# Cross-attention block on one core: one pair fewer turned on TensorE, later layer norm statistics, earlier fc weights, and weight sums at the head of their pair

## The chip, the core and the metric

The kernel runs on one core of a Trainium2 chip. The metric is the device time of one execution in microseconds (us); the median of several runs counts. The engines are named as in the profile: PE is TensorE, DVE is VectorE, ACT is ScalarE, POOL is GpSimd, SP is the engine that here only issues transfers.

## The reference

All data are float32. B = 4 batches, 512 queries and 512 keys of width D = 512, H = 16 heads of 32, and a hidden layer of 2048.

```
y = layer_norm(x)                     # ln1
q = y @ q_w + q_b;  k = ctx @ k_w + k_b;  v = ctx @ v_w + v_b
attn = softmax(mask(q k^T / sqrt(32)))
h = (attn v) @ cproj_w + cproj_b + x
out = h + gelu(layer_norm(h) @ fc_w + fc_b) @ proj_w + proj_b
```

## The kernel before, in words

**Windows, units and pairs.** The 16 heads of a batch make 4 groups, so there are 16 windows w = 4 * batch + group. A window has four query tiles qt of 128; unit u is 4 * w + qt, 64 in all. Two units make a pair: pair p is window p // 2, half p % 2. In this text "(w,qt)" names a unit and batch numbers count from 0, so "batch two" of the change is batch 1.

**One unit.** `scores` (L227) multiplies one query tile with all keys for four heads into PSUM (tile `sc`, one buffer), DVE adds the mask and takes the minimum (L239, output `s`), and ACT takes the exponential with the row sum (L243). The probabilities must then be transposed for the product with v. `turn` (L247) does this in one of two ways. For most pairs DVE transposes blocks of 32x32 (L271, tile `tb`), and when the pair is full its reciprocal sums are added (L276 to L279) and `copies` (L299) issues 16 transfers on SP (L313) that move the blocks to their places in `pT`. For the pairs listed in `ON_PE`, TensorE transposes instead (L257, tile `tpp`), DVE and ACT copy the result out of PSUM (L260, L262), and `turn_sums` (L326) transposes the sums (tile `tpr`).

**Where a pair is put.** `pT` has one buffer, so `exchange` (L288) lets only one pair at a time hold it (list `held`) and makes the next wait until `attend` (L336) has used it. A pair listed in `IN_G` goes into the buffer `gt` instead, which later holds the hidden layer and, at the end, fc's weights; it doesn't wait for `pT`. `attend` of pair p runs at the start of unit 2p + 4, except for the pairs that `AT` places by hand. Its product is tile `av` (L356).

**The order of the other work.** All engines follow the program's order (the schedule is written by hand). Into the units, each window w spreads the list `first[w]` (from its third unit on also `later[w]`): the projections `prep_k`, `prep_q`, `prep_v` of coming windows, the layer norm of coming batches, the output projection `cproj` and the first two batches' MLP. Each entry has a cost (3.4 for a chain of matmuls, 0.5 for a turn of the layer norm, 0 for the rest), and every unit takes entries twice, before and after its `turn`, while half of the next cost fits into the share due. `inputs(b)` returns four groups for batch b: x1 loads x, x2 is layer norm 1 in three parts (statistics of tiles 0 and 1; statistics of tiles 2 and 3 with the reciprocal root on POOL; the four normalizations L127), x3 is four turns (transposes L136 on PE, eviction with weight and bias on ACT or DVE, L139 and L141), x4 loads the context. `hid_` loads the residual of batch 0 on the current queue and has POOL add a bias to it (L368); `cproj` adds its product to that tile on DVE (L397).

**Queues.** Loads go through `Q[0]`: POOL's queue in windows 0 to 3, SP's from window 4 on. `load_mlp` (L440) loads as many MLP weights as its 8 buffers take, and is called again after each chain.

**The last two batches' MLP.** `last_mlps` (L513) multiplies 2x2 blocks with seven instead of eight products, from sums of blocks. `fc_pair` (L547) does this for two of fc's 16 weight blocks at a time (8 pairs c per batch): seven products of two matmuls each on PE, sums of the products on DVE, gelu on ACT. The products need sums of the weights: `sum_wa` (L509, four DVE instructions, L487 and L490) makes those of pair c + 1 while pair c runs, and `load_wa` (L505) loads those of pair c + 2 when pair c has been issued, into one of two buffers in `gt`.

Of the kernel before, what the change touches and what calls it, by code (L numbers as in the profile page):

```python
# [56 lines left out]
AHEAD = 3  # L57
NORMAL = 2
LAG = 4
IN_G = (2, 5)  # L60
IN_XE = (29, 31)
AT = {7: 1, 9: 2, 13: 4, 15: 5}
ON_PE = (0, 3, 6)
MW = 8
WARM = 14
PW = 2 * NT * HG * HD
# [7 lines left out]
def xattn_block(ctx: ExitStack, tc: tile.TileContext, x, encT, mask, q_w, k_w, v_w, c_w, fc_w, p_w, vecs, rows, out):  # L74
# [32 lines left out]
    def acc_tile(name):  # L107
        return ps_acc.tile([P, D], F32, tag="acc", name=name)
# [71 lines left out]
    def load_w(w, queue=None, names=("wk", "wq", "wv")):  # L180

        if w >= NW:
            return
        g = w % NG
        for n, src in (("wk", k_w), ("wq", q_w), ("wv", v_w)):
            if n in names:
                S[n, w] = (two if n == "wk" else one).tile([P, ND, P], F32, tag=n, name=f"{n}_{w}")
                (queue or Q[0]).dma_start(out=S[n, w], in_=src[:, g, :, :])

    def prep_k(w):  # L190
        b, g = divmod(w, NG)
        kT = kqp.tile([P, L], F32, tag="kT", name=f"kT_{w}")
        acc = acc_tile(f"acck_{w}")
        for d in range(ND):
            nc.tensor.matmul(acc, S["wk", w][:, d, :], eT[:, d, :], start=(d == 0), stop=(d == ND - 1))  # L195
        nc.scalar.activation(kT, acc, AF.Identity, bias=vec[:, KB + g : KB + g + 1], scale=1.0)
        S["kT", w] = kT

    def prep_q(w):
        b, g = divmod(w, NG)  # L200
        qT = kqp.tile([P, L], F32, tag="qT", name=f"qT_{w}")
        acc = acc_tile(f"accq_{w}")
        for d in range(ND):
            nc.tensor.matmul(acc, S["wq", w][:, d, :], xT[:, d, :], start=(d == 0), stop=(d == ND - 1))  # L204
        load_w(w + 1, names=("wq",))

        nc.scalar.activation(qT, acc, AF.Identity, bias=qb[:, g : g + 1], scale=-scale)
        S["qT", w] = qT
# [38 lines left out]
    def turn(w, qt):  # L247

        half, q = divmod(qt, 2)
        if 2 * w + half in ON_PE:  # L250
            if q == 0:
# [36 lines left out]
    def exchange():  # L288

        while waiting:  # L290
            w, half = waiting[0]
            if 2 * w + half not in IN_G + IN_XE:
                if held:
# [5 lines left out]
    def copies(w, half):  # L299
        tb = S["tb", w, half]  # L300

        pair = 2 * w + half
        if pair in IN_G or pair in IN_XE:
            pT = (gt if pair in IN_G else xe).rearrange("p (i n) -> p i n", i=NI)
        else:
# [10 lines left out]
    def over_sums(w, half):  # L316

        if 2 * w + half not in ON_PE:
            return
# [6 lines left out]
    def turn_sums(w, half):  # L326
        if 2 * w + half not in ON_PE:
            return
        tp = acc_tile(f"tpr_{w}_{half}")
        for q in range(2):  # L330
            nc.tensor.transpose(tp[:, ts(q, P)], S["rr", w, half][:, ts(q, P)], ident)
        rb = one.tile([P, 2 * P], F32, tag="rb", name=f"rb_{w}_{half}")
        nc.scalar.copy(rb, tp[:, : 2 * P])
        S["rb", w, half] = rb

    def attend(w, half):  # L336
# [4 lines left out]
        v, pT = S["v", w], S["pT", w, half]  # L341
        on_pe = 2 * w + half in ON_PE
        av = acc_tile(f"av_{w}_{half}")
# [26 lines left out]
    def load_hid(b, ts_):  # L370

        for t in ts_:
            if ("hid", b, t) not in S:
                S["hid", b, t] = hids.tile([P, D], F32, tag="hid", name=f"hid_{b}_{t}")
            Q[0].dma_start(out=S["hid", b, t], in_=S["xa", b][ts(t, P), :] if b else x[b, ts(t, P), :])
        for t in ts_:
            add_row(S["hid", b, t], 1 if b else 0)
# [135 lines left out]
    def last_mlps():  # L513
# [10 lines left out]
        def half_tile(name):  # L524
            return ps_last.tile([P, 2, HL], F32, tag="half", name=name)

        def acc_half(name):
            return acc_tile(name).rearrange("p (i l) -> p i l", i=2)

        def add(engine, o, x0, x1):  # L530
            engine.tensor_tensor(o, x0, x1, ALU.add)

        def y_blocks(b):
            return [S["yT", b][:, 2 * k : 2 * k + 2, j * HL : (j + 1) * HL] for k in range(2) for j in range(2)]

        def p_sums(c):

            c = slice(c, c + 2)
            b11, b12, b21, b22 = (pb[:, c, k, j * HL : (j + 1) * HL] for k in range(2) for j in range(2))
            b_sums(b11, b12, b21, b22, pt[:, 0, c], pt[:, 1, c], b12, pt[:, 2, c])  # L540
# [6 lines left out]
        def fc_pair(b, c, sums):  # L547
            a11, a12, a21, a22 = (wa[c % 2][:, i, 2 * k : 2 * k + 2] for i in range(2) for k in range(2))
            y11, y12, y21, y22 = y_blocks(b)
            s1, s2, s3, s4 = (ws[c % 2][:, i] for i in range(4))  # L550
            t1, t2, t3, t4 = (ys[:, i] for i in range(4))
            q1, q62 = (acc_half(f"{n}_{b}_{c}") for n in ("q1", "q62"))
            q75, q43 = (half_tile(f"{n}_{b}_{c}") for n in ("q75", "q43"))
            p1 = ring.tile([P, HL], F32, tag="p1", name=f"p1_{b}_{c}")
            uc, u34, h = (ring.tile([P, 2, HL], F32, tag=n, name=f"{n}_{b}_{c}") for n in ("uc", "u34", "h"))

            def product(o, a, y):
                for k in range(2):
                    nc.tensor.matmul(o, a[:, k], y[:, k], start=(k == 0), stop=(k == 1))  # L559

            def gelu(i, j, src):
                f = 2 * c + i
                nc.scalar.activation(
                    ga[:, c, i, j * HL : (j + 1) * HL], src, AF.Gelu_apprx_tanh,
                    bias=vec[:, FCB + f : FCB + f + 1], scale=1.0,
                )

            product(q1[:, 0], a11, y11)
            nc.scalar.copy(p1, q1[:, 0])
            product(q62[:, 1], a12, y21)  # L570
            product(q43[:, 1], s4, y22)
            product(q62[:, 0], s2, t2)
            add(nc.vector, uc, q62, p1[:, None, :].broadcast_to([P, 2, HL]))
            gelu(0, 0, uc[:, 1])
            product(q75[:, 0], s3, t3)
            product(q75[:, 1], s1, t1)
            add(nc.vector, u34, q75, uc[:, :1].broadcast_to([P, 2, HL]))
            add(nc.vector, uc[:, 0], q75[:, 1], u34[:, 0])
            gelu(1, 1, uc[:, 0])
            sums()  # L580
            product(q43[:, 0], a22, t4)
            add(nc.vector, h, q43, u34)
            gelu(1, 0, h[:, 0])
            gelu(0, 1, h[:, 1])
# [62 lines left out]
        for b in range(NORMAL, B):  # L647
# [15 lines left out]
            def sums(b=b):  # L663
                if b == NORMAL:
                    for c in range(0, NP, 2):
                        p_sums(c)
                if b + 1 < B:
                    load_hid(b + 1, range(NT))
# [16 lines left out]
    def do(fn):  # L685
        return [(0.0, fn)]

    def A(w):
        if w >= NW:
            return []  # L690
        return do(lambda: load_w(w + 1, names=("wk",))) + [
            (CHAIN, lambda: prep_k(w)),
            (CHAIN, lambda: prep_q(w)),
            (CHAIN, lambda: prep_v(w)),
        ]

    def C(b):
        return [(CHAIN, lambda t=t: cproj(b, t)) for t in range(NT)]
# [4 lines left out]
    def turns2(b):  # L703
        return [(TURN, lambda d=d: ln2_turn(b, d)) for d in range(ND)]
# [7 lines left out]
    def inputs(b):  # L712
        ln = [(0.0, lambda part=part: ln1(b, part)) for part in range(3)]
        return do(lambda: load_x(b)), ln, turns1(b), do(lambda: load_enc(b))
# [38 lines left out]
    first = [[] for _ in range(NW)]  # L753
    later = [[] for _ in range(NW)]
    x1, x2, x3, x4 = inputs(1)
    load2, k2, q2, v2 = A(2)
    load3, k3, q3, v3 = A(3)
    load4, k4, q4, v4 = A(4)
    first[0] = do(lambda: load_w(2, names=("wk",))) + [(CHAIN, lambda: prep_v(1)), (CHAIN, lambda: prep_q(1))] + x1 + [load2, k2, q2]
    first[1] = x2[:1] + [v2] + x2[1:2] + [load3, k3] + x2[2:] + [q3] + x3[:2] + [v3] + x3[2:] + x4  # L760
    first[2] = [load4, q4, k4, v4] + A(5)[:2]
    first[3] = A(5)[2:] + A(6)
    mlp = []
    for p in range(NORMAL):
# [6 lines left out]
    def hid_(b, *ts_):  # L771
        return do(lambda: load_hid(b, ts_))
# [17 lines left out]
    x1, x2, x3, x4 = inputs(2)  # L790
    first[3] += x1
    load, k, q, v = A(7)
    c, t2 = C(0), turns2(0)
    first[4] = do(load_mlp) + [load, k] + x2[:2] + [q] + x2[2:] + [v] + x3[:2] + x4 + hid_(0, 0, 1, 2, 3)
    later[4] = c[:1] + x3[2:] + c[1:] + rs(0)
    load, k, q, v = A(8)
    first[5] = norm(0, 0, 1) + [load, q] + norm(0, 2, 3) + [k] + t2 + [v] + do(lambda: proj_bias(0)) + some(5)
    load, k, q, v = A(9)
    x1, x2, x3, x4 = inputs(3)
    first[6] = [load, k, q] + some(5) + [v] + x1  # L800
    load, k, q, v = A(10)
    first[7] = [load, k, q] + some(5) + [v]

    load, k, q, v = A(11)
    first[8] = ct(1) + [load, k] + x2[:1] + [q] + x2[1:2] + some(1) + x2[2:] + [v] + x3[:2] + x4
    c = C(1)
    later[8] = c[:1] + x3[2:] + c[1:]
    load, k, q, v = A(12)
    first[9] = [load, q] + some(2) + [k] + some(3) + [v]
    load, k, q, v = A(13)  # L810
    first[10] = [load, k, q] + some(5) + [v] + yn(1)
    load, k, q, v = A(14)
# [4 lines left out]
    load, k, q, v = A(15)  # L817
    c = C(2)
# [98 lines left out]
```

## Time and profile before

| | |
|---|---|
| median of 3 runs | 842.71 us (839.12 to 842.92) |
| profiled execution: its time, its span | 844.56 us, 842.7 us |
| mean granted TensorE clock | 0.994 |
| PE busy | 818.0 us (97%) |
| DVE busy | 551.0 us (65%) |
| ACT busy | 345.0 us (41%) |
| POOL busy | 104.8 us (12%) |
| transposes of pairs on TensorE (L257) | 96 records, 282 ns each |
| block transposes on DVE (L271) | 232, 684 ns each |
| transfers of pairs on SP (L313, to pT) | 400 of 136 KB, 2.4 us to landing |

The span runs from the first to the last instruction of the profiled execution. A busy time is the time in which the engine had an instruction under way; those of PE overlap, so the starts of two instructions tell more than the length of one. The number in brackets at the end of a line of the timeline is the idle time before that work and what ended it.

### The profile page before, as it was taken

What the parts mean: (1) busy time and instruction counts of PE and PEld (TensorE: products, weight loads), DVE (VectorE), ACT (ScalarE), POOL (GpSimd) and SP (SyncE); (2) the same over time, 40 slices, a digit from 0 to 9 for tenths busy, and PEclk for the clock granted to TensorE, in tenths of its full rate; (3) what the DMA queues carried; (4) which work ended last, traced back from release to release, by engine and by line L of the source; (5) the groups of instructions that cost most, each with busy time, mean ns of one, the idle gap of its engine ahead of it and who ended that gap; (6) DMA issues with size and microseconds to landing.
All of it is one profiled execution on the core that took longest, in us unless ns stands there. A gap on an engine that the chain in (4) does not pass through costs nothing.

```text
span 842.7 us, 12030 instructions
## 1 busy us (share of the span) xinstructions
PE 818.0 (97%) x4098; PEld 476.6 (57%) x4098; DVE 551.0 (65%) x1254; ACT 345.0 (41%) x745; POOL 104.8 (12%) x124
## 2 busy tenths in 40 slices
PE   9988999989999999999999999999998999999998
PEld 7545555535444554354454444444446788887887
DVE  3595959596766686766886576777136886358511
ACT  2655555336663663456334285556002321023200
POOL 2311212222000021000100310000203012100011
PEclk9998999999999999999999999999999999999999
DMA  5455574957767686886769697857726450022001
GB/s 204 164 146 133 148 203 113 330 136 185 185 168 231 177 250 166 196 211 172 223 174 257 166 238 173 238 138 185 215 88 208 153 163 14 26 75 81 8 14 38
DMA packets 58909, 134.66 MB, mean 160 GB/s; under 512 B 11888, under 2 KB 14064, under 8 KB 58720
## 3 DMA queue, kind: packets, MB, share of 16 engines
q1 hardware_dynamic: 55440, 122.86, 53.6%
q0 software_dynamic: 2880, 9.90, 3.7%
q10 hardware_dynamic: 528, 1.14, 0.6%
q8 instruction: 33, 0.54, 0.3%
q14 instruction: 28, 0.23, 0.1%
HBM read 61.89 MB, written 7.34 MB: 82 GB/s over the span
## 4 chain that ended last, share of the span: by engine, by line
PE 83%; DVE 9%; DMA 4%; SPq 2%; issue 1%; ACT 1%; POOL 0%; DVEq 0%; ACTq 0%; POOLq 0%
PE accp L465 13%; PE accf L455 12%; PE av L356 7%; PE sc L234 7%; PE q L559 6%; PE accv L216 6%; PE acck L195 5%; PE accq L204 5%; PE accc L396 5%; SPq L313 2%; DVE gt L487 2%; PE q4p L595 2%; PE q3p L595 2%; PE q6p L595 2%; PE q1p L595 2%; PE q5p L595 2%
## 5 line engine op out<-in xcount | busy, mean ns | idle before, releaser
L243 ACT ACTIVATE s<-s,mn 128x512 f32<-128x512 f32 x256 | 181.7, 711 | 173.2 <-DVE mn L239 173.0
L239 DVE CUSTOM_DVE_ANT_0 s<-sc,mb 128x512 f32<-128x512 f32 x256 | 161.3, 686 | 49.9 <-PE sc L234 49.8
L271 DVE STREAM_TRANSPOSE tb<-s 128x512 f32<-128x512 f32 x232 | 147.7, 684 | 5.0 <-ACT s L243 5.0
L455 PE MATMUL accf<-yT,fcw 128*128 128x512 f32 x256 | 114.9, 599 | 0.0
L465 PE MATMUL accp<-pw,gt 128*128 128x512 f32 x256 | 114.3, 598 | 0.0
L455 PEld LDWEIGHTS accf<-yT,fcw 128*128 128x128 f32 x256 | 47.1, 190 | 65.0 <-issue 60.8
L465 PEld LDWEIGHTS accp<-pw,gt 128*128 128x128 f32 x256 | 47.4, 190 | 63.2 <-issue 60.7
L234 PE MATMUL sc<-kT,qT 32*128 32x512 f32 x512 | 73.2, 641 | 3.0 <-DVE mn L239 2.2
L356 PE MATMUL av<-pT,v 128*32 128x256 f32 x896 | 57.2, 398 | 7.4 <-DMA pT<-tb 4.9
L216 PEld LDWEIGHTS accv<-wv,xe 128*128 128x128 f32 x512 | 58.9, 192 | 8.9 <-issue 6.7
L216 PE MATMUL accv<-wv,xe 128*128 128x128 f32 x512 | 60.6, 277 | 0.0
L195 PE MATMUL acck<-xe,wk 128*128 128x512 f32 x128 | 58.7, 601 | 0.0
L559 PE MATMUL q<-ys,gt 128*128 128x256 f32 x256 | 57.9, 379 | 0.7 <-issue 0.7
L204 PE MATMUL accq<-xe,wq 128*128 128x512 f32 x128 | 58.5, 599 | 0.0
L396 PE MATMUL accc<-wc,oT 128*128 128x512 f32 x128 | 57.0, 597 | 0.0
L559 PE MATMUL q<-yT,gt 128*128 128x256 f32 x192 | 47.4, 385 | 5.6 <-DVE gt L487 5.5
L559 PEld LDWEIGHTS q<-ys,gt 128*128 128x128 f32 x256 | 48.6, 190 | 7.6 <-issue 1.0
L356 PEld LDWEIGHTS av<-pT,v 128*32 128x32 f32 x896 | 28.0, 113 | 37.4 <-issue 22.3
L243 ACT ACTIVATION_READ_ACCUMULATOR s<-s,mn 128x1 f32 x256 | 47.9, 187 | 0.0
L469 DVE TENSOR_TENSOR hid<-accp,hid 128x512 f32<-128x512 f32 x32 | 21.9, 685 | 39.7 <-PE accp L465 39.7
L223 POOL TENSOR_TENSOR v<-v,row 128x512 f32<-128x512 f32 x16 | 20.5, 1279 | 205.2 <-ACT v L221 205.0
L559 PEld LDWEIGHTS q<-yT,gt 128*128 128x128 f32 x192 | 35.3, 190 | 15.6 <-PE q L559 7.0
(121 smaller groups left out, 865.7 us busy)
## 6 DMA issues: line engine op xcount, KB each, us to landing
pT<-tb SPq DMA_DIRECT2D x400, 136.0 KB, 2.4
fcw<-fc_w_dram SPq DMA_DIRECT2D x32, 256.0 KB, 3.2
pw<-p_w_dram SPq DMA_DIRECT2D x32, 256.0 KB, 3.5
gt<-fc_w_dram SPq DMA_DIRECT2D x32, 256.0 KB, 2.8
gt<-tb SPq DMA_DIRECT2D x32, 136.0 KB, 3.4
pb<-p_w_dram SPq DMA_DIRECT2D x16, 256.0 KB, 3.8
xe<-tb SPq DMA_DIRECT2D x24, 136.0 KB, 2.4
xe<-encT_dram SPq DMA_DIRECT2D x12, 256.0 KB, 5.9
```

Of the source, the lines that this page charges most:

```text
L195: nc.tensor.matmul(acc, S["wk", w][:, d, :], eT[:, d, :], start=(d == 0), stop=(d == ND - 1))
L204: nc.tensor.matmul(acc, S["wq", w][:, d, :], xT[:, d, :], start=(d == 0), stop=(d == ND - 1))
L216: nc.tensor.matmul(acc[:, ts(t, P)], eT[:, d, ts(t, P)], S["wv", w][:, d, :], start=(d == 0), stop=(d == ND - 1),)
L234: nc.tensor.matmul(sc[:, h, :], qT[r, ts(qt, P)], kT[r, :], start=True, stop=True)
L239: nc.vector.tensor_tensor_reduce(out=s, in0=sc[:, h, :], in1=S["mb", w // NG], scale=1.0, scalar=FMAX, op0=ALU.add, op1=ALU.min, accum_out=mn,
L243: nc.scalar.activation(s, s, AF.Exp, bias=mn, scale=-1.0, accum_out=sums[:, qt, h : h + 1])
L271: nc.vector.transpose(tv[:, q, h], S["ps", w, qt][h])
L356: nc.tensor.matmul(av[ts(h, HD), : 2 * P].rearrange(shape, **kw), v[:, t, ts(h, HD)], p[t][h], start=(t == 0), stop=(t == NT - 1),)
L396: nc.tensor.matmul(acc, S["oT", b][:, g, ts(t, P)], wc[:, g, :], start=(g == 0), stop=(g == NG - 1))
L455: nc.tensor.matmul(acc, S["fcw", b, f][:, d, :], S["yT", b][:, d, :], start=(d == 0), stop=(d == ND - 1))
L465: nc.tensor.matmul(acc, gT[q % 2][:, k, ts(t, P)], S["pw", b, q * FQ + k], start=(k == 0), stop=(k == FQ - 1))
L559: nc.tensor.matmul(o, a[:, k], y[:, k], start=(k == 0), stop=(k == 1))
```

## The change

It makes five edits. The pair 6 (window 3, first half) leaves `ON_PE`, so it is transposed by DVE and moved by SP into `pT`. The pair 7 is put into `gt`. In window 1, the parts of layer norm 1 of batch 1 move behind other entries of the list, all four turns come after `prep_v(3)`, and the context's load stands ahead of them. The first eight MLP weights are loaded at the start of window 2 instead of window 4, which also puts them on POOL's queue instead of SP's. In `fc_pair` the sums of the next pair's weights stand first, and the product with s4 moves from the third to the sixth place in every pair but the first of a batch.

```
-IN_G = (2, 5)
+IN_G = (2, 5, 7)
...
-ON_PE = (0, 3, 6)
+ON_PE = (0, 3)
...
+            sums()
             product(q1[:, 0], a11, y11)
             nc.scalar.copy(p1, q1[:, 0])
             product(q62[:, 1], a12, y21)
-            product(q43[:, 1], s4, y22)
+
+            if c == 0:
+                product(q43[:, 1], s4, y22)
             product(q62[:, 0], s2, t2)
...
             gelu(1, 1, uc[:, 0])
-            sums()
+            if c:
+                product(q43[:, 1], s4, y22)
             product(q43[:, 0], a22, t4)
...
-    first[1] = x2[:1] + [v2] + x2[1:2] + [load3, k3] + x2[2:] + [q3] + x3[:2] + [v3] + x3[2:] + x4
-    first[2] = [load4, q4, k4, v4] + A(5)[:2]
+    first[1] = x2[:1] + [v2, load3, k3] + x2[1:2] + [q3] + x2[2:] + [v3] + x4 + x3
+    first[2] = do(load_mlp) + [load4, q4, k4, v4] + A(5)[:2]
...
-    first[4] = do(load_mlp) + [load, k] + x2[:2] + [q] + x2[2:] + [v] + x3[:2] + x4 + hid_(0, 0, 1, 2, 3)
+    first[4] = [load, k] + x2[:2] + [q] + x2[2:] + [v] + x3[:2] + x4 + hid_(0, 0, 1, 2, 3)
```

## The prediction

> **What bounds the kernel now.** I read the busy times first, then the waits of each engine, then the timelines of PE, DVE and SP around the edits.
>
> ```profile
> PE 818.0 (97%) x4098; PEld 476.6 (57%) x4098; DVE 551.0 (65%) x1254; ACT 345.0 (41%) x745; POOL 104.8 (12%) x124
> ```
>
> PE bounds the whole, so an edit gains what it takes off PE, or a hole that it closes in PE's row. The holes lie in three places. In window 1 and at pair 6 (PE, starts and lengths in us):
>
> ```profile
> 60.38 1.14 PE L234 MATMUL sc<-kT,qT 32*128 32x512 f32 x8 [2.18 <-DVE mn L239]
> ...
> 66.98 2.07 PE L257 MATMUL tpp<-ident,s 128*128 128x128 f32 x12 [1.83 <-ACT s L243]
> ...
> 112.84 0.66 PE L257 MATMUL tpp<-ident,s 128*128 128x128 f32 x4 [0.50 <-ACT qT L207]
> ...
> 120.04 1.91 PE L257 MATMUL tpp<-ident,s 128*128 128x128 f32 x16
> ```
>
> In window 4 PE waits twice for a pair's transfers:
>
> ```profile
> 155.05 1.93 PE L356 MATMUL av<-pT,v 128*32 128x256 f32 x32 [1.72 <-DMA fcw<-fc_w_dram]
> ...
> 177.85 3.39 PE L356 MATMUL av<-pT,v 128*32 128x256 f32 x32 [3.72 <-DMA pT<-tb]
> ```
>
> SP's own timeline tells why the second is late, and DVE's what else depends on SP there:
>
> ```profile
> 151.41 3.92 SPq L447 DMA_DIRECT2D fcw<-fc_w_dram  x8
> ...
> 157.42 3.09 SPq L149 DMA_DIRECT2D xe<-encT_dram  x4
> 161.35 2.20 SPq L375 DMA_DIRECT2D hid<-x_dram  x4
> ```
> ```profile
> 167.97 0.69 DVE L397 TENSOR_TENSOR hid<-accc,hid 128x512 f32<-128x512 f32 x1 [7.32 <-POOL hid L368]
> ```
>
> Pair 8's transfers follow only at 163.96, behind these loads and after pair 7 has given `pT` back. And DVE stands 7.32 us before batch 0's residual is loaded and biased; everything behind L397 on DVE stands too. At the end, PE waits in each pair of fc's weights for their sums:
>
> ```profile
> 644.42 1.13 PE L559 MATMUL q<-yT,gt 128*128 128x256 f32 x4 [1.80 <-DVE gt L487]
> ...
> 650.93 1.10 PE L559 MATMUL q<-yT,gt 128*128 128x256 f32 x4 [0.21 <-DVE gt L487]
> ```
>
> [...] it grants 0.50 from 68.95 to 75.75 us and from 178.2 to 181.5 us, after the holes above. [...] the blocks of (4,2) could be transposed at 162, and start at 170.22 behind L397. [...] 3.92 us of SP for eight loads; on POOL one issue takes 0.55 us.
>
> **Part by part.**
>
> *Layer norm in window 1.* The statistics of tiles 2 and 3 (2 x (0.66 + 0.18), 1.6 us start to start) leave the place ahead of L239 of (1,1), which starts at 56.2 instead of 57.8; PE's scores of (1,2) come at 58.8. They return ahead of L239 of (1,2), but the normalizations (1.8) leave there: it starts at 63.6 instead of 65.3, and tpp at 65.25 instead of 66.98: −1.7. From tpp to the scores of (2,0) PE took 83.37 − 66.98 = 16.4 us, 6.8 of them at half clock. With smaller holes I take full clock: −3.0 more (half of 6.8 is 3.4; waits give some back). The normalizations now stand ahead of L239 of (1,3), under PE's product for pair 1 and v: they end about when its scores do. Turns and context load only change places; the same counts, and POOL has nothing between: 0. If that cover went, the 1.8 us would be PE's. Sum −4.7, from −1.7 (clock falls anyway) to −4.7.
>
> *Weights earlier.* 8 x 0.55 = 4.4 us of POOL in window 2. Behind them in POOL's queue stand wk of window 5, wq, wv and v's bias (1.28 us each), none needed for 10 us; 2 MB beside a DMA share of 0.54 to 0.61. 0, at worst +1. On SP, eight issues go: priced below.
>
> *Pair 6.* PE loses two tpp groups of 1.75 us start to start, the 0.50 wait and the sums' 0.3: −4.3. DVE loses 4 copies of 0.69 and gains 8 transposes, 2.4 us per four, and 0.4 for sums: +2.4, beside at least 8 us of DVE idle time between 111 and 134; free. If DVE were full it would cost 2.4. SP gets 16 issues, 10.6 us. On the new clock pair 5's issues run 103.9 to 114.5, pair 6's blocks and sums are done at 115.1, issues end at 125.8, and the row of before gives 2.3 to 3.9 us to landing: 128.1 to 129.6. PE wants them at 136.94 − 4.7 − 4.3 − 0.3 = 127.6. A new wait of 0.5 to 2; I take 1.2. So the product for pair 6 starts at 128.8 instead of 136.94: −8.1.
>
> *Window 4: pair 8 passes the residual's load.* This is where I expect most of that to be lost. Pair 7 sits in `gt`, so `pT` is free when pair 8 is full, and `turn` of (4,1) issues its 16 transfers at once. The context's and the residual's loads are taken after that `turn`: on SP they move from ahead of pair 8 to behind it. Pair 8's sums ended at 155.7; DVE runs from scores (3,3) to there without a hole, so now at 147.4. Add 10.6 for pair 8, 3.1 for the context and 0.9 between: the residual's issue comes at 162, against 161.35 before, although all else is 8 us sooner. Landing took 5.3 with eleven weight loads ahead; with a lighter queue I take 3.5, then POOL's 1.27: L397 at **167.0**, against 167.97 (bounds 165.5 to 170).
>
> What waits: PE runs on through the output projection's tile 2, but tile 3 needs L397's PSUM buffer, so PE stands from about 161, and its clock falls. That is hidden: DVE needs 22.3 us from L397 to L239 of (5,1) (190.3 − 167.97), PE only some 21 even with the clock at half first. Before, PE came 0.8 later than DVE there because of the 3.72 wait and the half clock; both are gone. From L397 to the product for pair 9 it was 199.45 − 167.97 = 31.5 and is now 30.1: −1.4. With −1.0 for L397 itself: **−2.4 in all up to here**, not −8.1 and the waits too.
>
> *fc's pairs.* Seven products take 28 records of 0.216 us, 6.05 us; pairs take 6.4 to 8.1. Batch 2: 688.85 − 633.77 − 48.4 = 6.7 lost; batch 3: 790.72 − 739.16 − 48.4 = 3.2. The sums (1.5 us) were made from 5 to 7 us after a pair's start and wanted at 6.05 + 1.73 = 7.8. Now they wait only for the next weights: the last block is issued when the pair before ends, 3.0 us to landing, sums done at 4.6; after the sums of gelu's blocks (even pairs, 2.7) and a normalization, at 5.7. Both before 7.8. DVE's sum uc then waits behind them, from 2.6 to 4.6 or 6.4; who waits for it is ACT's gelu, wanted later, and PSUM, two pairs deep: 0. The first pair of batch 2 keeps some 0.9 for the sums of y. Gain 9.9 − 0.9 − 0.4 for what I can't see = **−8.6**; bounds 0 and −9.9. PE runs to the end of the chain, so all of it counts.
>
> Sum: 842.7 − 2.4 − 8.6 = 831.7. The profiled execution's own time (844.56) lies 1.9 above its span, and the median (842.71) on the span by chance; I give 831.7 for the median.
>
> **Rivals.**
>
> *No gate.* The residual lands in time, or DVE recovers. Then the −8.1 stays and the waits 1.72 and 3.72 and 1.7 of half clock go too: −15.2 − 8.6 gives 819. For it: the loads are free to start early. Against: SP's row, in order.
>
> *The end gives nothing.* The wait for sums turns into one for weights, as DVE stands for the load at the head of the pair: 842.7 − 2.4 = 840.3. It would take a landing of over 6 us (7.8 − 1.5 after the issue); 5.2 is the longest in batch 2, 3.0 the median. If only window 1's clock still falls, 834.7.
>
> *Slower, by the gate.* Each us that L397 comes after 169.4 is lost one for one. At the gain of 8.6 it decides from 178.0 on. If each of pair 8's 16 issues took as long as the longest L313 of before (2007 ns), they took 32 us and L397 came 21.5 later, at 188.5: 842.7 + 19.1 − 8.6 = 853. Against: the median issue is 0.59.
>
> **How the numbers follow.** Forecast 0.57, with its own range 828 to 836. No gate 0.17. The end gives nothing, or only the clock falls, 0.15. The slower gate 0.06. The last 0.05 is for what I don't see, on either side. The range 821 to 838 takes the forecast, the way to "no gate" but for its last 2 us, and the half-clock case. About 0.5% (4.2 us) is what a measurement can tell from no change: faster is the forecast, no gate and half of the third, 0.83; same 0.09; slower 0.08.
>
> **What would show it.** The rows L257, L260 and L262 at 64, 8 and 8; PE without 50% clock near 70; a wait of PE for pT near 128; on SP, pair 8's L313 ahead of L149 and L375; a wait of DVE for POOL at L397 of about 15 us and a hole in PE of 5 us or more near 161 to 167; in the pairs of fc no wait of PE for gt L487, and one of DVE for the transfers into gt of 1 to 3 us. I am wrong if L397 comes before 163 or after 170, or if pairs of fc still take over 6.2 us.

## The result and the profile after

| | before | after |
|---|---|---|
| median, us | 842.26 (839.12 to 845.02, 6 runs) | 836.84 (835.47 to 838.42, 6 runs) |
| profiled execution: time, span | 844.56, 842.7 | 838.42, 836.6 |

The ratio of after to before is 0.994, interval 0.9914 to 0.9966. The change makes the kernel faster by 5.4 us (0.6%); 11 were forecast. The direction held, and the median lies within the forecast's range (821 to 838). The size did not hold.

PE was busy for 5.3 us less than the 818.0 of before. The span became 6.1 us shorter:

```profile
PE 812.7 (97%) x4064; PEld 472.9 (57%) x4064; DVE 557.9 (67%) x1259; ACT 342.3 (41%) x740; POOL 109.5 (13%) x132
```

The timeline of PE after the change, at the places that were shown of before (start, length in us; in brackets the idle time before and what ended it):

```profile
59.35 1.14 PE L234 MATMUL sc<-kT,qT 32*128 32x512 f32 x8 [0.61 <-DVE mn L239]
65.72 2.16 PE L257 MATMUL tpp<-ident,s 128*128 128x128 f32 x12 [1.60 <-ACT s L243]
...
110.83 1.93 PE L356 MATMUL av<-pT,v 128*32 128x256 f32 x32 [1.15 <-DMA gt<-tb]
...
133.95 1.93 PE L356 MATMUL av<-pT,v 128*32 128x256 f32 x32 [1.51 <-DMA pT<-tb]
...
172.88 5.63 PE L396 MATMUL accc<-wc,oT 128*128 128x512 f32 x8 [6.70 <-DVE hid L397]
...
201.90 1.93 PE L356 MATMUL av<-pT,v 128*32 128x256 f32 x32
```

The last line is the product for pair 9, which started at 199.45 before the change.

The hole ahead of the scores at 59 us has shrunk from 2.18 to 0.61. Two waits are new, at the products for pair 4 (110.83) and pair 6 (133.95), for their transfers. The two waits in window 4 (1.72 and 3.72) are gone, and one of 6.70 stands in their place. What ends it is L397 on DVE. DVE's timeline, and POOL's for what DVE waits for:

```profile
172.14 0.69 DVE L397 TENSOR_TENSOR hid<-accc,hid 128x512 f32<-128x512 f32 x1 [15.82 <-POOL hid L368]
```
```profile
170.84 4.93 POOL L368 TENSOR_TENSOR hid<-hid,row 128x512 f32<-128x512 f32 x4 [19.96 <-DMA hid<-x_dram]
```

DVE stands for 15.8 us because POOL stands for 20, and POOL waits for the residual's load. SP's timeline says where that load was:

```profile
120.44 10.56 SPq L313 DMA_DIRECT2D pT<-tb  x16
135.29 13.09 SPq L313 DMA_DIRECT2D gt<-tb  x16
...
152.88 11.36 SPq L313 DMA_DIRECT2D pT<-tb  x16
164.29 2.02 SPq L149 DMA_DIRECT2D xe<-encT_dram  x4
166.36 1.85 SPq L375 DMA_DIRECT2D hid<-x_dram  x4
```

The 16 transfers of pair 8 (152.88) stand ahead of the residual (166.36). Before the change they stood behind it (163.96 behind 161.35). So L397 is reached 4.2 us later than before (172.14 against 167.97), although PE was ahead of its old times until then, by 3.0 us at pair 6's product.

In fc's pairs of batch 2, PE's timeline has lost its brackets for `gt`:

```profile
643.44 1.89 PE L559 MATMUL q<-yT,gt 128*128 128x256 f32 x8
645.30 2.86 PE L559 MATMUL q<-ys,gt 128*128 128x256 f32 x12
647.99 1.03 PE L559 MATMUL q<-yT,gt 128*128 128x256 f32 x4
...
649.72 1.89 PE L559 MATMUL q<-yT,gt 128*128 128x256 f32 x8
```

Batch 2's eight pairs take 49.49 us instead of 55.08, batch 3's 48.35 instead of 51.56: −8.8 together. The product for pair 9 starts at 201.90 instead of 199.45: +2.45. With −8.8 that makes −6.35, nearly the whole of the span's −6.1.

### The profile page after: what moved, and what is told of

Same layout as the page of the kernel before. It is cut to its first block, busy times and chain, and to the rows that moved or that the text cites. A ratio compares the mean times of both kernels' runs of the same rounds, so it can differ in the third digit from the quotient of the medians.

```text
span 836.6 us, 11984 instructions
## 1 busy us (share of the span) xinstructions
PE 812.7 (97%) x4064; PEld 472.9 (57%) x4064; DVE 557.9 (67%) x1259; ACT 342.3 (41%) x740; POOL 109.5 (13%) x132
## 3 DMA queue, kind: packets, MB, share of 16 engines
q10 hardware_dynamic: 528, 1.14, 0.6%
## 4 chain that ended last, share of the span: by engine, by line
PE 82%; DVE 7%; DMA 4%; SPq 3%; POOL 1%; issue 1%; ACT 0%; DVEq 0%; ACTq 0%; POOLq 0%
PE accp L465 13%; PE accf L455 12%; PE q L559 12%; PE sc L234 7%; PE av L356 6%; PE accv L216 5%; PE accq L204 5%; PE acck L195 5%; PE accc L396 3%; DVE s L239 2%; SPq L313 2%; DVE tb L271 2%; DMA xn<-x_dram 2%; PE q4p L599 2%; PE q3p L599 2%; PE q5p L599 2%
## 5 line engine op out<-in xcount | busy, mean ns | idle before, releaser
L239 DVE CUSTOM_DVE_ANT_0 s<-sc,mb 128x512 f32<-128x512 f32 x256 | 161.2, 686 | 47.9 <-PE sc L234 47.8
L271 DVE STREAM_TRANSPOSE tb<-s 128x512 f32<-128x512 f32 x240 | 152.6, 684 | 6.1 <-ACT s L243 5.0
L396 PE MATMUL accc<-wc,oT 128*128 128x512 f32 x128 | 59.2, 614 | 6.7 <-DVE hid L397 6.7
L559 PE MATMUL q<-ys,gt 128*128 128x256 f32 x256 | 60.3, 380 | 0.7 <-issue 0.7
L356 PE MATMUL av<-pT,v 128*32 128x256 f32 x864 | 53.9, 391 | 4.5 <-DMA pT<-tb 3.2
L396 PEld LDWEIGHTS accc<-wc,oT 128*128 128x128 f32 x128 | 24.4, 196 | 39.5 <-issue 31.0
```

The costliest lines, as they stand in the source:

```text
L239: nc.vector.tensor_tensor_reduce(out=s, in0=sc[:, h, :], in1=S["mb", w // NG], scale=1.0, scalar=FMAX, op0=ALU.add, op1=ALU.min, accum_out=mn,
L271: nc.vector.transpose(tv[:, q, h], S["ps", w, qt][h])
L356: nc.tensor.matmul(av[ts(h, HD), : 2 * P].rearrange(shape, **kw), v[:, t, ts(h, HD)], p[t][h], start=(t == 0), stop=(t == NT - 1),)
L396: nc.tensor.matmul(acc, S["oT", b][:, g, ts(t, P)], wc[:, g, :], start=(g == 0), stop=(g == NG - 1))
```

## The experiments

Each kernel was measured beside the kernel before on the same chip (whose median was 842.1 to 842.4), and its ratio is to that kernel. The changed kernel's 836.84 was measured earlier, beside a median of 842.26. The theory is the gate: the residual stands behind pair 8 on SP, L397 comes late, and PE stands. Its first rival is that window 1 and its clock hold the missing time.

**1. The residual ahead of pair 8** (the changed kernel with one list entry moved):

```
-    first[4] = [load, k] + x2[:2] + [q] + x2[2:] + [v] + x3[:2] + x4 + hid_(0, 0, 1, 2, 3)
+    first[4] = [load, k] + x2[:2] + [q] + x2[2:] + hid_(0, 0, 1, 2, 3) + [v] + x3[:2] + x4
```

> The changed kernel with one edit: batch 0's residual is loaded in unit (4,1) ahead of v of window 7, so on SP it stands ahead of pair 8's 16 transfers instead of behind them and the context. Theory (SP's order holds DVE at L397): the residual's issue comes near 150 instead of 166.4 us, L397 near 157 instead of 172.1, DVE's 15.8 us wait and PE's 6.7 us hole go, and the scores of (5,1) come some 12 us sooner; 836.8 - 12 = about 825 us. Rival (the hole is DVE's or the transfers' own load, and the place of the residual in the queue matters little): L397 moves, but the next wait takes its place within a few us, 833 to 837.

Measured: 822.83 us, ratio 0.9769 (0.9743 to 0.9794). SP's and DVE's timelines of this kernel:

```profile
145.52 1.85 SPq L375 DMA_DIRECT2D hid<-x_dram  x4
...
150.28 10.21 SPq L313 DMA_DIRECT2D pT<-tb  x16
```
```profile
154.45 0.69 DVE L397 TENSOR_TENSOR hid<-accc,hid 128x512 f32<-128x512 f32 x1 [0.74 <-PE accc L396]
```

Now DVE waits for PE at L397, 0.74 us, and not for POOL. L397 comes 17.7 us sooner and PE's hole of 6.70 is gone. Some 3 us of this are the clock in window 1 (an estimate: about half of the 6.8 us that the changed kernel's profile has at 0.50), which stayed full in this profile (1.00 from 58.29 to 71.94); against experiment 6's profile, where it did so too, L397 comes 15.1 us sooner. The place of this one load, with POOL's bias additions behind it, costs the change 14.0 us of median (836.84 − 822.83).

**2. fc's edit alone** (the kernel before, with the sums first in `fc_pair` and the product with s4 moved):

```
+            sums()
             product(q1[:, 0], a11, y11)
...
-            product(q43[:, 1], s4, y22)
+            if c == 0:
+                product(q43[:, 1], s4, y22)
...
-            sums()
+            if c:
+                product(q43[:, 1], s4, y22)
```

> The kernel before with the edit of fc's pairs alone. Theory (the end gains as the two traces show, 55.1 to 49.5 us and 51.6 to 48.4 us, and the rest of the change loses): 842.3 - 8.8 = 833.5 us, less than the changed kernel. Rival (the end's gain depends on the rest): 836 to 842.

Measured: 834.07 us, ratio 0.9897 (0.9872 to 0.9921): −8.05. The end gives what was forecast; the loss lies in the rest. Whether the earlier sums or the later product with s4 does it was not tried apart.

**3. The earlier weights alone** (the kernel before):

```
-    first[2] = [load4, q4, k4, v4] + A(5)[:2]
+    first[2] = do(load_mlp) + [load4, q4, k4, v4] + A(5)[:2]
...
-    first[4] = do(load_mlp) + [load, k] + ...
+    first[4] = [load, k] + ...
```

> The kernel before with the earlier load of the first eight MLP weights alone. Theory (SP's order in window 4 sets the time): eight issues, about 4 us, leave SP ahead of the context and the residual; L397 at about 163.5 instead of 168, pair 8's transfers start near 158.6 instead of 164, PE's wait of 3.72 us and the half clock behind it go: about 836.5 us. Rival (those transfers are bound by the bytes, which are only moved): 841 to 842.

Measured: 836.05 us, ratio 0.9925 (0.9904 to 0.9946): −6.07. SP's and DVE's timelines:

```profile
150.36 1.85 SPq L149 DMA_DIRECT2D xe<-encT_dram  x4
152.25 2.47 SPq L375 DMA_DIRECT2D hid<-x_dram  x4
155.93 24.11 SPq L313 DMA_DIRECT2D pT<-tb  x22
```
```profile
160.26 0.69 DVE L397 TENSOR_TENSOR hid<-accc,hid 128x512 f32<-128x512 f32 x1 [1.13 <-PE accc L396]
```

Without the eight weight loads ahead of it the residual's issue comes at 152.25 instead of 161.35, DVE no longer waits for POOL at L397, and pair 8, now issued at 155.93 instead of 163.96, is no longer late. Here too some 3 us are the clock's, which stayed full in window 1 (1.00 from 56.47 to 70.12). Experiment 2's kernel has the old order on SP, and in its profile the clock stayed full there too (1.00 from 58.78 to 72.43): against it the residual's issue comes 6.6 us sooner (158.89 there) and L397 6.15 (166.41). So the gate was already there in the kernel before, and this part alone opens it. In the whole change it is shut again by another part.

**4. The changed kernel with the old arrangement of pairs 6 and 7, in parts.** Pair 6 back on TensorE and 7 back in `pT`:

```
-IN_G = (2, 5, 7)
+IN_G = (2, 5)
...
-ON_PE = (0, 3)
+ON_PE = (0, 3, 6)
```

> The changed kernel with both edits of the pairs undone (pair 6 on TensorE again, pair 7 in pT); it keeps fc's pairs, the earlier weights and the layer norm. Theory (the pairs' edits put the residual behind pair 8 and lose more than they gain): the parts add up, 842.3 - 8.1 (fc's pairs) - 6.1 (earlier weights) - 1.8 (layer norm) = 826.3 us, 10 less than the changed kernel. Rival (the residual would be late anyway): 834 to 841.

Measured: 826.39 us, ratio 0.9814 (0.9794 to 0.9834). Only pair 7 back in `pT`:

```
-IN_G = (2, 5, 7)
+IN_G = (2, 5)
```

> The changed kernel with pair 7 taken out of gt again: one number less in IN_G, pair 6 stays with DVE and SP. Pair 8 must then wait for pair 7 in pT, so SP issues the context and the residual ahead of it. Theory: the residual's issue comes near 153 instead of 166.4 us, L397 at about 160, DVE's wait of 15.8 us goes; pair 8's transfers come after 153 and may leave 1 to 2 us of waiting at its product: 825 to 827 us. Rival (it is pair 6's 16 transfers on SP that delay all): 834 to 837.

Measured: 822.98 us, ratio 0.9773 (0.9752 to 0.9793). Only pair 6 back on TensorE:

```
-ON_PE = (0, 3)
+ON_PE = (0, 3, 6)
```

> The changed kernel with pair 6 back on TensorE, pair 7 still in gt. Theory (the place of pair 8 in SP's queue decides, and moving pair 6 off TensorE is worth 4.3 us less the two waits of 1.2 and 1.5 us that it brought, all of it ahead of L397): PE's waits near 110 and 133 us go, the DVE wait at L397 stays over 13 us, and the time is 838.0 us. Rival (pair 6's transfers make the residual late): 828 to 832.

Measured: 838.2 us, ratio 0.9945 (0.9929 to 0.9961). The timelines of SP and DVE with pair 7 in `pT`:

```profile
146.26 1.85 SPq L149 DMA_DIRECT2D xe<-encT_dram  x4
148.15 2.65 SPq L375 DMA_DIRECT2D hid<-x_dram  x4
151.29 29.26 SPq L313 DMA_DIRECT2D pT<-tb  x31
```
```profile
155.47 0.69 DVE L397 TENSOR_TENSOR hid<-accc,hid 128x512 f32<-128x512 f32 x1 [2.33 <-POOL hid L368]
```

and of DVE and PE with pair 6 on TensorE and pair 7 still in `gt`:

```profile
170.59 0.69 DVE L397 TENSOR_TENSOR hid<-accc,hid 128x512 f32<-128x512 f32 x1 [13.97 <-POOL hid L368]
```
```profile
171.33 6.02 PE L396 MATMUL accc<-wc,oT 128*128 128x512 f32 x8 [4.67 <-DVE hid L397]
```

A pair 7 in `pT` holds pair 8 back, so the two loads are issued in the meantime, and L397 comes at 155.47. With pair 7 in `gt` the gate is shut whichever way pair 6 goes. So the number 7 in `IN_G` costs 13.9 us with pair 6 off TensorE (836.84 − 822.98) and 11.8 with it on (838.2 − 826.39). Taking pair 6 off TensorE is worth 3.4 where the gate is open (826.39 − 822.98) and 1.4, with intervals that overlap, where it is shut.

**5. Layer norm's edit alone** (experiment 4's kernel with pair 7 in `pT`, and the old list of window 1):

```
-    first[1] = x2[:1] + [v2, load3, k3] + x2[1:2] + [q3] + x2[2:] + [v3] + x4 + x3
+    first[1] = x2[:1] + [v2] + x2[1:2] + [load3, k3] + x2[2:] + [q3] + x3[:2] + [v3] + x3[2:] + x4
```

> The kernel e7_no_gt7 (pair 7 in pT) with the order of layer norm 1 in window 1 as it was before. There PE's clock stays full in window 1 in most executions, so this shows the edit's own worth. Theory (1.8 us of DVE work leave the way of the scores, and the 3.0 us of half clock that the prediction counted were one execution's): 823.0 + 1.8 = 824.8 us. Rival (the order also spares the clock's fall in most executions): 827 to 828.

Measured: 823.83 us, ratio 0.9787 (0.9774 to 0.98), 0.85 above 822.98; the intervals overlap, so by the medians the edit may be worth nothing. In the traces PE goes from the scores of (1,0) to those of (2,0) in 31.91 us with the old list and in 30.06 with the new (in experiment 7's first kernel, whose window 1 is that of experiment 4's), both at full clock (pair 1's product took 1.93 us in both, and 3.64 at half clock in the changed kernel): −1.85. Why the medians show less stays open.

**6. Work for PE in the hole of window 1** (the changed kernel with seven 128x128 products of the identity ahead of the transposes of (1,2), to keep the clock up; nothing reads them):

```
+                for _ in range(FILL if (w, qt, h) == (1, 2, 0) else 0):
+                    nc.tensor.matmul(tp[:, :P], ident, ident, start=True, stop=True)
```

> The changed kernel with 7 matmuls of the identity (about 1.5 us, output overwritten) put ahead of the transposes of (1,2), where PE waits 1.6 us for ACT. Theory (that hole makes the clock fall at 67.6 us): the clock stays full until 160 us, the scores of (2,0) come 3 us sooner, and as all until L397 follows, 833.8 us. Rival ([...] the hole at 58.7 counts): the clock still falls, 836.8.

Measured: 836.96 us, ratio 0.9928 (0.9905 to 0.9951), as much as without. The clock stayed full in window 1 (1.00 from 55.95 to 69.60) and pair 6's product came at 130.73 instead of 133.95. But DVE still stood 15.69 us at L397 (L400 in this kernel), and PE waited for it:

```profile
169.58 0.69 DVE L400 TENSOR_TENSOR hid<-accc,hid 128x512 f32<-128x512 f32 x1 [15.69 <-POOL hid L371]
```
```profile
170.33 6.21 PE L399 MATMUL accc<-wc,oT 128*128 128x512 f32 x8 [6.40 <-DVE hid L400]
...
202.32 1.93 PE L359 MATMUL av<-pT,v 128*32 128x256 f32 x32
```

L397 came 2.6 us sooner than in the changed kernel (169.58 against 172.14). But the clock fell again in two places, by the lengths of the products: the eight at 170.33 took 6.21 us, and the scores at 189.95 took 2.09 (the profile's mean clock of 0.992 leaves room for two falls of 6.8 us). In the changed kernel's profile only the first of these is slow (5.63 at 172.88; eight such products take 3.60 at full clock, and the scores at 192.36 took 1.14), and the product for pair 9 came 0.4 later than there (202.32 against 201.90). Nothing was left of the 3 us. So the fall of the clock in window 1 does not by itself hold the missing time. The run doesn't show that the products held the clock, since experiment 1's kernel kept the full clock without them (last section).

**7. Better homes for the waits of pairs 4 and 6.** First, later products (experiment 1's kernel):

```
-AT = {7: 1, 9: 2, 13: 4, 15: 5}
+AT = {7: 1, 9: 2, 14: 4, 15: 5, 17: 6}
```

> The kernel e1_hid (residual loaded ahead of pair 8) with the products of pairs 4 and 6 one unit later each (AT: 14 for pair 4, 17 for pair 6). Theory (PE's two waits for their transfers, 1.3 and 2.4 us, are new costs of the change that one unit of delay covers): 822.8 - 3.7 = 819.1 us. Rival (pair 6's transfers start later too, as pT comes free a unit later, and the wait only moves): 822 to 824.

Measured: 824.91 us, ratio 0.9787 (0.9763 to 0.9811). Both waits are gone and PE has a new one at pair 7:

```profile
146.67 3.64 PE L356 MATMUL av<-gt,v 128*32 128x256 f32 x32 [1.39 <-DMA wk<-k_w_dram]
```

The wait moved to the next pair, and the clock fell there, by the product's length: 3.64 us, where pair 6's at 136.00 took 1.93 (mean clock 0.996). Then, half of the transfers of pairs 4 and 6 issued by ACT (experiment 4's kernel with pair 7 in `pT`):

```
-                q = nc.scalar if w == NW - 1 and half and i % 2 else nc.sync
+                q = nc.scalar if (pair == 2 * NW - 1 or pair in (4, 6)) and i % 2 else nc.sync
```

> The kernel e7_no_gt7 with half of the 16 transfers of pairs 4 and 6 issued by ACT instead of SP. Theory (PE's new waits for these pairs, 1.06 and 1.51 us, come from SP's 10 us of issuing): the last one lands 3 to 5 us sooner, both waits go, 820.4 us. Rival (ACT's instructions behind the issues wait, or the bytes bound the transfers): 823 to 825.

Measured: 835.84 us, ratio 0.9938 (0.9919 to 0.9957), 12.9 worse than its base. The rival had named the mechanism, but neither forecast had the size. ACT's and PE's timelines:

```profile
91.65 7.55 ACTq L313 DMA_DIRECT2D pT<-tb  x8
99.24 0.37 ACT L333 COPY rb<-tpr 128x256 f32<-128x256 f32 x1 [9.22 <-DMA pT<-tb]
```
```profile
102.56 2.09 PE L234 MATMUL sc<-kT,qT 32*128 32x512 f32 x8 [6.36 <-DVE mn L239]
```

Eight issues held ACT for 7.55 us. Evictions and exponentials stood behind them for 9.2, and PE, waiting for its turn, for 6.36.

**The parts together.** From 842.3: fc's pairs −8.05, earlier weights −6.07, layer norm −0.85, pair 6 off TensorE −3.4, pair 7 in `gt` +13.9 gives 837.8; measured 836.84. The last two are differences to the changed kernel itself, so the sum tests only the first three: they give 827.3, and the kernel with just these three measured 826.39. The best kernel is the change without pair 7 in `gt`, or with the residual ahead of pair 8: 823, 2.3% below the kernel before.

## Why the prediction was right in its mechanism and wrong in its size

*fc's pairs: right.* −8.8 in the trace against −8.6, −8.05 by medians, and the pairs take 6.19 and 6.04 us. The detail held in batch 3: DVE waits for the weights four times, 1.4 to 1.9 us (1 to 3 were forecast), and the sums of the second to the seventh pair end 4.4 to 5.0 us into a pair (4.6 and 5.7). In batch 2 DVE was fuller than I thought. It waits once, 1.01, and the sums end 4.5 to 6.2 us into the third to the seventh pair and 7.1 into the second (650.56 − 643.44), where PE wanted them only 0.9 later.

*The gate: right in kind, wrong in size. This is the step that failed.* Pair 8 passes the residual on SP, DVE waits some 15 us (15.82), PE stands over 5 (6.70), and from L397 on DVE sets the pace: 22.23 us to L239 of (5,1) (forecast 22.3) and 29.8 to the product for pair 9 (30.1). But L397 came at 172.14, not 167.0, past the 170 that I had named as the limit. Of L397's −1.0 it makes +4.2, and of the −2.4 up to pair 9's product +2.45; by the medians the change without fc's part is +2.6. (The forecast had 147.4 for pair 8 where 155.7 − 8.1 is 147.6, and 167.0 where its sum is 166.8; the two slips cancel.) In the profiled execution the 5.1 us come from these, in order:

- *The −3.0 for a full clock in window 1.* The clock fell again, at 67.6 instead of 68.95. I put the fall of before down to the holes ahead of it and expected smaller ones to end it. That was my estimate, and it failed: the holes went from 2.18 and 1.83 to 0.61 and 1.60, and the clock fell after 3.41 us with PE busy for 1.75, as before after 1.86. The fall came in some executions and not in others: experiments 2 and 3 have the same order of work in window 1, and their profiles show none. I counted it as a gain. From the scores of (1,0) to those of (2,0) the change saved 1.9 us, not 4.7 (+2.8); the execution also came 0.55 later to these scores.
- *Pair 4's wait (+1.15).* I took pair 6 for the only pair with new trouble. The transposes of pair 6 on TensorE had stood ahead of pair 4's product and hidden its transfers. With them gone PE waits there too. With pair 6 on TensorE there is no such wait, and in the kernels without it there is (1.06, 1.29).
- *Pair 6's wait*: 1.51 for 1.2, and 0.3 that I can't place. So pair 6's product starts at 133.95, not 128.8, and pair 8's issue at 152.88, not 147.4. Here 0.3 more is lost.
- *Pair 8 to the residual*: 13.5 us instead of 14.6 (−1.1). *Landing*: 4.5 us after the issue instead of 3.5 (+1.0).

So up to L397 some 3 of the profile's 5 us are the clock's. The clock doesn't explain the median, though. Two executions of the changed kernel had a mean clock of 0.996, which leaves room for one fall of 6.8 us (0.004 of 834 us is 3.3, about half of 6.8; the profiled one, with two, had 0.991), and they still took 835.5 and 835.8 us. In experiment 6's profile window 1 had the full clock, L397 came at 169.58, and the gain was lost behind it: from L397 to pair 9's product it took 32.7 us, where I had 30.1 with one fall of the clock, and here there were two. So a us saved at L397 was not a us saved at the end. Nor does the median of before hold the 3 us: its executions with a mean clock of 0.998 have a median of 842.06 (11 runs), those with 0.994 or less 842.49 (20 runs).

By the medians the miss of 5.1 us divides in two. With the gate open the kernel takes 822.83 (experiment 1), 3.8 more than the 819 of "no gate": what I counted as gained ahead of the gate was too much. Two waits of PE in that profile, which I had at nothing (pair 4, 1.29) and at 1.2 (pair 6, 2.37), are 2.5 of it. The rest stays open. And the gate takes 14.0 us, 1.3 more than the 12.7 between the forecast and "no gate".

Among the rivals, "no gate" (819) and "the end gives nothing" (840.3) are refuted by the 15.82 at L397 and by the −8.8. "Only the clock still falls" (834.7) came nearest, 2.1 us off, though experiment 6 speaks against its reason.

*The earlier weights: wrong as a part.* I gave them 0 by themselves. Alone they are worth 6.07, because in the kernel before they stood ahead of the residual on the very queue that I had named as the gate. In the whole change it did not show, since pair 7 in `gt` takes the same microseconds back.

*Layer norm* had −1.7 for the order of DVE's work; the traces show −1.85, the medians −0.85 with overlapping intervals. *Pair 6* had −4.3 of PE and a wait, net −3.1; where the gate is open it is worth 3.4.

*Of the signs named:* L257, L260 and L262 are at 64, 8 and 8. SP's order, DVE's wait and PE's hole are as said, some 5 us later. The full clock near 70 did not come in the profiled execution.

## What to carry to other kernels

When a buffer comes free sooner, look at what its producer issues next and what stands behind that on the same queue: here one pair with a buffer of its own put 16 transfers ahead of a small load, and the gain of four other edits was cut from 19 us to 5. Before you count a clock's fall as a cost that an edit removes, ask whether other executions of the same kernel have it, and whether a later wait would take the gain back; and when you take work off an engine, list each wait that this work had been covering, not only those of the pair that you moved. Price a part also as if it were made alone: a part worth nothing in the sum can be the one that opens the gate.

## What the runs showed of the hardware

*The clock fell after a stretch in which PE was half busy, in some executions and not in others.* Up to 200 us the two main profiles grant 0.50 four times: from 68.94 to 75.75 and from 178.18 to 181.59 before, from 67.57 to 74.40 and from 169.97 to 176.80 after. The shortest of these is 3.41 us long, and the busy times here are taken over stretches of that length. PE was busy for 0.33 us of the one ahead of 178.18, and for 0.00 of the one ahead of 169.97. In window 1 PE was busy for half of it. Busy times by stretch (start:end, length, then PE, PEld, DVE, ACT, POOL; then the granted clock), of the kernel after, of fc's edit alone and of experiment 1:

```profile
64.16:67.57 3.41, 1.75 (x12) 1.26 (x12) 2.88 (x10) 2.71 (x7) 1.80 (x3) 1.00 0.89 204
67.57:70.99 3.42, 2.89 (x23) 1.51 (x24) 1.67 (x4) 1.74 (x5) 0.00 (x0) 0.50 1.02 290
```
```profile
65.61:69.02 3.41, 1.90 (x12) 1.25 (x12) 2.88 (x9) 2.87 (x9) 0.42 (x1) 1.00 0.91 251
69.02:72.43 3.41, 2.79 (x37) 2.08 (x40) 1.59 (x3) 2.36 (x5) 0.00 (x0) 1.00 1.04 253
```
```profile
61.70:65.11 3.41, 1.80 (x5) 0.52 (x4) 3.34 (x10) 1.00 (x3) 1.50 (x3) 1.00 0.69 157
65.11:68.53 3.42, 2.71 (x24) 1.74 (x28) 1.60 (x6) 3.42 (x9) 0.30 (x1) 1.00 0.88 249
```

After 1.75 us of PE in a stretch (of the kernel before: 1.86) the next is at half clock. After 1.90 us, and after 1.80 us that were a few long products and not short transposes, it is not. PE's busy time alone does not decide it: in the kernel before the clock did not fall after 1.73 us of PE (58.70 to 62.11), and fell after 1.86 (65.53 to 68.94). The fall in window 1 is in three of the twelve profiles (before, after, and pair 6 on TensorE with pair 7 in `gt`), with the old list of layer norm and with the new. What decides it was not shown.

*Eight issues took 7.55 us of ACT.* ACT took 0.94 us for each of pair 4's transfers (7.55 / 8, experiment 7's second kernel), SP 0.66 for each of pair 6's in the kernel after (10.56 / 16). ACT's 7.55 us were lost to the engine that makes the exponentials.

*Four of DVE's sums took 5.7 us while POOL was adding, and 1.5 us while it was not.* The timelines of DVE and POOL in fc's first pair of the kernel after:

```profile
640.93 1.49 DVE L490 TENSOR_TENSOR gt<-gt 128x256 f32<-128x256 f32 x1
642.35 4.30 DVE L487 TENSOR_TENSOR gt<-gt 128x256 f32<-128x256 f32 x3
```
```profile
640.66 5.70 POOL L368 TENSOR_TENSOR hid<-hid,row 128x512 f32<-128x512 f32 x4
```

The four sums take 5.7 us beside POOL's four additions, also 5.7. At 649 us, where POOL does nothing, the same four take 1.5 (0.41 and 1.21). Why they took longer was not shown. It cost nothing here, as PE did not wait for the sums.
